# Selective-scan kernel: one three-set product on VectorE, a shared ring of three PSUM slots, five places for sets

## The chip, the cores and the metric

One core of a Trainium2 chip runs the whole program in one launch. The metric is device microseconds of that core; the time of a kernel is the median of its runs. A profile is one more execution of the same program, taken by the hardware profiler; its durations and waits belong to that execution and not to the median.

## What is computed

Two layers of a 2-D state-space block over 8 images of 64x64 positions and 96 channels. Each layer normalizes by groups of channels, projects 96 channels to 192 (and to 192 gates), convolves each channel 3x3, and then scans the 4096 positions in four directions (by rows, by columns, and both backward). Cut to what matters, layer 0's scan is, per direction, channel and one of 16 states:

```
delta = softplus(dt + bias)              # per position and channel
dA    = exp(delta * A)                   # the decay, one per state
h     = dA * h + delta * u * B[state]    # along the positions
y     = sum over states of h * C[state]
```

The four directions' y are added, normalized, gated and projected back. Layer 1 does the same with a form of the scan in which only the first 160 positions of a direction can matter for these inputs (its decays fall below any float after them); the kernel calls these *short* sets, and keeps a general second layer behind a test on the data that does not run here.

## The kernel before

**Tiling.** A *set* is 128 partitions by 1024 positions in float32: 32 channels times 4 of the 16 states. Four sets (`i` = 0 to 3) make a *group*: all 16 states of 32 channels. Three groups make a *job* (96 channels), two jobs a *unit* (192 channels, 1024 positions of one direction), and 16 units an image: 4 directions of 4 pieces. So an image has 96 groups and the program 768 groups of long sets, and 48 short sets (6 for each image).

**What one group costs each engine.** With lines as in the profile:

- ScalarE (ACT) writes each set's decay into a PSUM slot of 128x1024 (two banks): `fill`, L939. Once a group it copies delta\*u, which a DMA has spread over the partitions, into PSUM too: `drive`, L957. It also copies the finished sums out (`release`, L1074) and keeps the last state of each set (`keep_state`, L1003).
- VectorE (DVE) multiplies delta\*u by the tables of B, for sets 0 and 1 in one instruction of 128x2048 (L977) and for set 2 in one of 128x1024 (L979), and runs one scan instruction per set (L992), in place over the product.
- GpSimd (POOL) forms the product with B for set 3 (`early`, L965), and multiplies every scanned set by C into a tile `out` (`read_out`, L1008). Once a job it also forms delta\*u (`take_product`, L603).
- TensorE (PE) sums the four states in a partition group and the four sets into one PSUM bank (`collect`, L1035 and L1044), and in between does the projections, the softplus sums and the convolutions of other images (L573, L693, L727, L1111).
- SyncE (SP) issues the DMAs: `fetch` (L532) brings delta and delta\*u of each group, two groups ahead, 512 KB each; `replicate` (L543) brings the eight tables of B and C of a unit, 512 KB each.

**The products lie in a ring** of four places of one SBUF tile, `ring[:, i, :]`: set `i` of every group has place `i`. The tables lie in one SBUF tile, B's at 0 to 3 and C's at 4 to 7, and are overwritten in place at each new unit. `out` has 5 buffers.

**PSUM.** Eight banks: two decay slots (`pslot`, 2 buffers of two banks), one slot for delta\*u and for the short sets' gates (`pdrive`, two banks), one bank for the sums (`pacc`), one for everything else (`pmisc`).

**The order is written out by hand**: no scheduler moves an instruction, and each engine runs its instructions in the order in which the loop of `scan_rows` (L455) issues them. The loop steps over the sets; at the step of set n it issues

1. on SP, the fetch for the group that begins at set n+5;
2. on DVE, `advance_set` of set n: the products, if n is set 0 (L977) or set 2 (L979) of its group, and then the scan;
3. on ACT, `fill` of set n+1, then, if set n+2 begins a group, `drive` of that group; then `release` of the group that ended at set n-4, `keep_state` of set n-1, and `gate` of set n+1 if that is short;
4. on POOL, `read_out` of set n-1, and after it `early` of set n+2 if that is set 3 of its group;
5. on SP, the tables of the unit that begins at set n+4, n+3, ... n: B0 and B1 together four sets ahead, then C0 and B3, then C1 and B2, then C2, then C3, each after the last reader of the old table;
6. on PE, `collect` of set n-3, and a plan of stages of the next jobs, on all engines.

So on POOL a group's order is: read-out of set 0, product of set 3, read-outs of sets 1, 2 and 3; the job's `take_product` stands between the read-out of set 3 and the next group's read-out of set 0. The last scan of a group (set 3) needs POOL's product; each read-out needs its scan; a product on DVE needs the read-outs of what lay in its places; a fill needs the scan that last read its slot; a read-out needs the `collect` that last read its `out` buffer.

Of the kernel before, what the change touches and what calls it, by code (L numbers as in the profile page):

```python
# [9 lines left out]
F32 = mybir.dt.float32  # L10
AF = mybir.ActivationFunctionType
ALU = mybir.AluOpType
PSUM = bass.MemoryType.PSUM
# [8 lines left out]
T = 1024  # L22
# [3 lines left out]
P = 128  # L26
# [3 lines left out]
NG = C // GC  # L30
NS = N // GS
# [2 lines left out]
ROWS = R + 1 + 2 * N  # L34
PE_ROWS = 40
AHEAD = 5
SETS = 4
PER = NG * NS
HEAD = 160
HN = K * HEAD  # L40
# [5 lines left out]
HT = 2 * BLOCK  # L46
# [6 lines left out]
def two_ss2d_layers(ctx: ExitStack, tc: tile.TileContext, t: dict, out: bass.AP):  # L53
# [13 lines left out]
    nc = tc.nc  # L67
# [40 lines left out]
    for i in range(L // MM):  # L108
        at = slice(i * MM, (i + 1) * MM)
# [277 lines left out]
    def scan_parts(b):  # L387

        units, jobs, sets = [], [], []
        for k in range(K):
            order = range(NT) if k < 2 else range(NT - 1, -1, -1)
            for nth, i in enumerate(order):
                unit = dict(k=k, nth=nth, t0=i * T, column=k % 2 == 1, backward=k >= 2)
                unit.update(short=False, n=T)
                units.append(unit)
                for h in range(NH):  # L400
                    jobs.append(dict(unit=unit, h=h))
                    for g in range(NG):
                        group = dict(unit=unit, job=jobs[-1], h=h, g=g)
                        sets += [
                            dict(unit=unit, group=group, i=i, first=h == g == i == 0)
                            for i in range(NS)
                        ]
        if b >= 1:
            unit, more_jobs, more = short_parts(b - 1)
            units, jobs, sets = units + [unit], jobs + more_jobs, sets + more  # L410
        x_dbl = [dram.tile([2 * ROWS, L], F32, name=f"x_dbl{c}", bufs=2) for c in "rc"]
        return units, jobs, sets, x_dbl
# [12 lines left out]
    def scan_rows(xc, y, parts, plan, rows, beside):  # L425

        with (
            tc.tile_pool(name="loads", bufs=2, side="right") as loads,
            tc.tile_pool(name="piece", bufs=1) as piece,
            tc.tile_pool(name="work", bufs=2) as work,
            tc.tile_pool(name="pslot", bufs=2, space=PSUM) as pslot,  # L440
            tc.tile_pool(name="pdrive", bufs=1, space=PSUM) as pdrive,
            tc.tile_pool(name="pacc", bufs=1, space=PSUM) as pacc,
            tc.tile_pool(name="pmisc", bufs=1, space=PSUM) as pmisc,
        ):
            units, jobs, sets, x_dbl = parts
            total = len(sets)
            plan = plan(pmisc)
            with tc.manual_schedule():
                state = None
                arena = piece.tile([P, 4 * T], F32, name="arena")  # L450
                ring = work.tile([P, SETS, T], F32, name="set", bufs=1)
                tables = loads.tile([P, 2 * NS, T], F32, name="bc_rep", bufs=1)
                cums = cycle(tables[:, i, :] for i in (1, 3, 2, NS + 1))
                plan.setdefault(-1, []).insert(0, lambda: low_rows(x_dbl, units[1], rows))
                for n in range(-AHEAD, max(total + 4, max(plan, default=0) + 1)):  # L455
                    at = lambda i: sets[n + i] if 0 <= n + i < total else None
                    m, j = divmod(n + 1, PER)
# [12 lines left out]
                    fetch(at(AHEAD), False, loads, None)  # L470
                    fetch(at(2), True, loads, cums)
                    if at(0) and at(0)["unit"]["nth"] == 0 and at(0)["first"]:
                        state = piece.tile([P, D // GC * NS], F32, name="state0", bufs=2)
                    advance_set(at(0), state, ring, tables)
                    fill(at(1), pslot)
                    drive(at(2), pdrive)
                    release(at(-4), y, beside)
                    keep_state(at(-1))
                    gate(at(1), pdrive)
                    early(at(1), True, ring)  # L480
                    read_out(at(-1), work)
                    early(at(2), False, ring)
                    replicate(at(4), x_dbl, tables, ("b", 0), ("b", 1))
                    replicate(at(3), x_dbl, tables, ("c", 0), ("b", 3))
                    replicate(at(2), x_dbl, tables, ("c", 1), ("b", 2))
                    replicate(at(1), x_dbl, tables, ("c", 2))
                    replicate(at(0), x_dbl, tables, ("c", 3))
                    replicate_short(at(4), "b", tables[:, 0, :])
                    replicate_short(at(3), "c", tables[:, NS, :])
                    late = (n + 1) % NS == 0  # L490
                    if not late:
                        collect(at(-3), xc, y, pacc)
                    for stage in plan.pop(n, []):
# [444 lines left out]
        rate = w["a0"][:, rate : rate + 1]  # L938
        nc.scalar.activation(s["decay"], s["group"]["dt"], AF.Exp, scale=rate)  # L939

    def gate(s, pdrive):

        if s and s["unit"]["short"]:
            s["gate"] = pdrive.tile([P, T], F32, name="drive")[:, :HT]

            for i in range(NS):
                rate = w["a1_half"][:, column(s) + i :][:, :1]
                cum, out = blocks(s["group"]["cum"], i), blocks(s["gate"], i)  # L950
                nc.scalar.activation(out, cum, AF.Tanh, bias=half_log, scale=rate)  # L951

    def drive(s, pdrive):

        if s and s["i"] == 0 and not s["unit"]["short"]:
            s["group"]["drive"] = pdrive.tile([P, T], F32, name="drive")[:, : s["unit"]["n"]]
            nc.scalar.copy(s["group"]["drive"], s["group"]["dtu"])  # L957

    def early(s, short, ring):

        if s and by_gpsimd(s) and s["unit"]["short"] == short:
            nth = s["group"]["h"] * NG + s["group"]["g"] if short else s["i"]
            s["buf"] = ring[:, nth % SETS, : s["unit"]["n"]]
            b = s["unit"]["b", s["i"]]
            nc.gpsimd.tensor_tensor(s["buf"], s["group"]["dtu"], b, ALU.mult)  # L965

    def advance_set(s, state, ring, tables):
# [2 lines left out]
            return  # L970
        unit = s["unit"]
        if not by_gpsimd(s):
            i = s["i"]
            s["buf"] = ring[:, i, :]
            if i == 0:
                drive = s["group"]["drive"].unsqueeze(1).broadcast_to([P, 2, T])
                nc.vector.tensor_tensor(ring[:, :2, :], drive, tables[:, :2, :], ALU.mult)  # L977
            elif i > 1:
                nc.vector.tensor_tensor(s["buf"], s["group"]["drive"], unit["b", i], ALU.mult)  # L979
        if unit["short"]:  # L980
            buf = s["buf"]
            nc.vector.scalar_tensor_tensor(  # L982
# [21 lines left out]

    def read_out(s, work):
        if s:
            s["out"] = work.tile([P, T], F32, name="out", bufs=5)[:, : s["unit"]["n"]]
            nc.gpsimd.tensor_tensor(s["out"], s["buf"], s["unit"]["c", s["i"]], ALU.mult)  # L1008

    def collect(s, xc, y, pacc):  # L1010
# [239 lines left out]
    def scan_last(b, xc):  # L1250

        unit, jobs, sets = short_parts(b)
        with (
# [21 lines left out]
                            at, at, w["dsum1"][:, h : h + 1], None, ALU.mult  # L1275
                        )
            with (
                tc.tile_pool(name="pslot", bufs=2, space=PSUM) as pslot,
                tc.tile_pool(name="pdrive", bufs=1, space=PSUM) as pdrive,
                tc.tile_pool(name="pacc", bufs=2, space=PSUM) as pacc,  # L1280
                tc.manual_schedule(),
            ):
# [3 lines left out]
                for n in range(-4, len(sets) + 4):  # L1286
# [2 lines left out]
                    fetch(at(2), True, loads, cums)  # L1289
                    replicate_short(at(3), "c", tables[:, 1, :])  # L1290
                    advance_set(at(0), None, ring, tables)
                    fill(at(1), pslot)
                    gate(at(1), pdrive)
                    early(at(1), True, ring)
                    read_out(at(-1), work)
                    collect(at(-2), xc, xc, pacc)
# [760 lines left out]
```

## Time and profile before

| | |
|---|---|
| three runs | 11965.03, 11974.39, 11977.57 us; median 11974.39 us |
| the profiled execution | 11977.88 us, of which the span is 11976.1 us |
| granted TensorE clock, mean | 0.758 |
| first group of images 0 to 7 starts at | 138.0, 1506.9, 2984.7, 4455.5, 5919.7, 7391.5, 8855.7, 10320.8 us in the trace |
| image 2's scans, 2973.3 to 4231.0 us of the span: busy | DVE 1197.30, POOL 1181.86, ACT 980.63 of 1257.70 us |
| ACT fill (L939), mean of 3072 | 1114 ns |
| DVE scan with a carried state (L992), mean of 2304 | 2340 ns |
| DVE scan from zero (L992), mean of 768 | 2281 ns |
| POOL read-out (L1008), mean of 3072 | 2371 ns |
| POOL product for set 3 (L965), mean of 768 | 2419 ns |
| POOL delta\*u (L603), mean of 240 | 2644 ns |
| ACT drive (L957), mean of 768 | 1013 ns |

The page lists busy time by engine and the costliest groups of instructions, with the idle time of the engine ahead of them and what ended it. The view of waits totals, for each pair of lines, how long one waited for the other. The timeline lists instructions in order of time; equal neighbours are merged into one line with a count ("x2"), and a wait stands in brackets behind the instruction that it held up, with its releaser. A wait for several semaphores is put down to the one that came last.

### The profile page before, as it was taken

The page shows a single profiled execution, that of the slowest core. Times are in us where ns is not written, and L with a number is a line of the kernel's source. Part 1 is how long each engine was busy: PE and PEld are TensorE (multiplying, and loading weights), DVE is VectorE, ACT ScalarE, POOL GpSimd, SP SyncE. Part 2 cuts the span into 40 slices and gives each one's busy share as a digit, 9 for nine tenths or more (in the row PEclk, how much of TensorE's full clock was granted, in tenths as well). Part 3 has the DMA queues.
Part 4 walks back from the last instruction along what each step waited for, and adds up shares of the span by engine and source line. Part 5 has one row for each costly group of instructions (what it writes and reads, how often), then busy time and mean ns, then how long its engine had stood idle before and what let it go on. Part 6 is the DMA issues. An engine that isn't in the chain of part 4 may idle for free. (4 is left out here: it accounts for less than half of the span.)

```text
span 11976.1 us, 146959 instructions
## 1 busy us (share of the span) xinstructions
PE 8766.6 (73%) x50950; PEld 3994.0 (33%) x50950; DVE 10805.4 (90%) x6095; ACT 9033.1 (75%) x14768; POOL 10621.1 (89%) x4799
## 2 busy tenths in 40 slices
PE   6865577777877777877787777877677776886557
PEld 2332233332333323333233332333233332333322
DVE  8999899996999979999799987999879998899985
ACT  6777678776787767877778777787777877777775
POOL 6999799996999969999799987999879998799984
PEclk7776677777777777777777777777777877777667
DMA  4444444544445445444444445444544554444441
GB/s 132 154 167 156 130 160 165 166 161 146 159 160 167 161 146 170 165 159 156 150 165 165 167 145 162 164 156 167 166 144 166 167 166 160 143 155 164 157 147 62
DMA packets 670703, 1862.39 MB, mean 156 GB/s; under 512 B 186728, under 2 KB 201486, under 8 KB 669949
## 3 DMA queue, kind: packets, MB, share of 16 engines
q1 hardware_dynamic: 662781, 1840.30, 46.7%
q10 hardware_dynamic: 7168, 12.59, 0.3%
q8 instruction: 405, 6.64, 0.2%
q14 instruction: 349, 2.86, 0.1%
HBM read 1539.34 MB, written 313.28 MB: 155 GB/s over the span
## 5 line engine op out<-in xcount | busy, mean ns | idle before, releaser
L1008 POOL TENSOR_TENSOR out<-set,bc_rep 128x1024 f32<-128x1024 f32 x3120 | 7318.7, 2369 | 624.8 <-DVE set L992 531.0
L992 DVE TENSOR_TENSOR_SCAN set<-decay,state,set 128x1024 f32<-128x1024 f32 x2304 | 5322.6, 2340 | 314.5 <-ACT decay L939 172.3
L939 ACT ACTIVATE decay<-dt_rep,w_a 128x1024 f32<-128x1024 f32 x3072 | 3420.5, 1114 | 1277.0 <-DVE set L992 1272.3
L1044 PE MATMUL acc<-out,w_gather 128*32 128x256 f32 x24576 | 2405.7, 519 | 50.3 <-POOL out L1008 49.9
L1111 PE MATMUL ps_conv<-edged,taps 96*96 96x512 f32 (+1 forms) x4032 | 2222.8, 695 | 19.3 <-DVE arena L865 9.7
L965 POOL TENSOR_TENSOR set<-dtu_rep,bc_rep 128x1024 f32<-128x1024 f32 (+1 forms) x816 | 1966.4, 2410 | 70.8 <-DMA dtu_rep<-dtu_short 38.6
L992 DVE TENSOR_TENSOR_SCAN set<-decay,set 128x1024 f32<-128x1024 f32 x768 | 1731.4, 2281 | 122.6 <-ACT decay L939 60.6
L977 DVE TENSOR_TENSOR set<-drive,bc_rep 128x2048 f32<-128x2048 f32 x768 | 1743.4, 2270 | 35.7 <-DMA bc_rep<-x_dblr 24.1
L727 PE MATMUL ps_sp<-w_eye,arena 128*96 128x128 f32 x7680 | 1122.4, 309 | 584.2 <-ACT arena L739 489.3
L1035 PE MATMUL acc<-map,w_eye 96*32 96x256 f32 x4608 | 578.0, 585 | 1309.8 <-ACT map L1074 859.6
L1074 ACT COPY map<-acc 32x256 f32<-32x256 f32 x3072 | 1472.6, 479 | 68.7 <-PE acc L1044 27.9
L1044 PEld LDWEIGHTS acc<-out,w_gather 128*32 128x32 f32 x24576 | 880.5, 141 | 1435.3 <-issue 1043.0
L727 PEld LDWEIGHTS ps_sp<-w_eye,arena 128*96 128x96 f32 x7680 | 972.4, 144 | 893.1 <-ACT arena L739 607.7
L693 PE MATMUL ps_dt<-w_dtw,x_dbl 7*128 7x96 f32 x3840 | 832.8, 382 | 572.4 <-ACT arena L739 460.4
L1111 PEld LDWEIGHTS ps_conv<-edged,taps 96*96 96x96 f32 (+1 forms) x4032 | 708.3, 190 | 1305.9 <-issue 1249.8
L693 PEld LDWEIGHTS ps_dt<-w_dtw,x_dbl 7*128 7x128 f32 x3840 | 727.2, 279 | 821.1 <-ACT arena L739 530.0
L979 DVE TENSOR_TENSOR set<-drive,bc_rep 128x1024 f32<-128x1024 f32 x768 | 922.0, 1201 | 30.9 <-DMA bc_rep<-x_dblr 14.2
L957 ACT COPY drive<-dtu_rep 128x1024 f32<-128x1024 f32 x768 | 777.9, 1013 | 109.6 <-DMA dtu_rep<-dtu_far 85.0
L704 ACT ACTIVATE arena<-ps_dt 128x384 f32<-128x384 f32 x480 | 235.1, 490 | 580.2 <-PE ps_dt L693 552.3
L1035 PEld LDWEIGHTS acc<-map,w_eye 96*32 96x32 f32 x4608 | 104.3, 125 | 1631.2 <-ACT map L1074 1005.3
L603 POOL TENSOR_TENSOR arena<-arena,map 96x1024 f32<-96x1024 f32 x240 | 634.7, 2644 | 7.9 <-ACT arena L739 7.8
L1003 ACT COPY state<-set 128x1 f32<-128x1 f32 x2304 | 422.3, 183 | 6.8
(207 smaller groups left out, 7991.9 us busy)
## 6 DMA issues: line engine op xcount, KB each, us to landing
dt_rep<-dt_far SPq DMA_DIRECT2D x768, 512.0 KB
dtu_rep<-dtu_far SPq DMA_DIRECT2D x768, 512.0 KB
bc_rep<-x_dblr SPq DMA_DIRECT2D x512, 512.0 KB
bc_rep<-x_dblc SPq DMA_DIRECT2D x512, 512.0 KB
dt_far<-arena SPq DMA_DIRECT2D x240, 384.0 KB
dtu_far<-arena SPq DMA_DIRECT2D x240, 384.0 KB
xc_far<-conv_out SPq DMA_DIRECT2D x224, 192.0 KB
dt_rep<-dt_short SPq DMA_DIRECT2D x48, 480.0 KB
```

The lines of the kernel that those rows point to most:

```text
L693: nc.tensor.matmul(job["ps"][:, j, :], unit["x_dbl"][: R + 1, at : at + P], w["dtw0"][:, k, h * C : (h + 1) * C], start=True, stop=True,)
L727: nc.tensor.matmul(job["ps"][:C, j * P : (j + 1) * P], job[name][:, s * BLOCKS + j, :], w["whole_eye"], is_transpose=True, start=i == 0, s ...
L939: nc.scalar.activation(s["decay"], s["group"]["dt"], AF.Exp, scale=rate)
L957: nc.scalar.copy(s["group"]["drive"], s["group"]["dtu"])
L965: nc.gpsimd.tensor_tensor(s["buf"], s["group"]["dtu"], b, ALU.mult)
L977: nc.vector.tensor_tensor(ring[:, :2, :], drive, tables[:, :2, :], ALU.mult)
L979: nc.vector.tensor_tensor(s["buf"], s["group"]["drive"], unit["b", i], ALU.mult)
L992: nc.vector.tensor_tensor_scan(ordered(s["buf"], unit), ordered(s["decay"], unit), ordered(s["buf"], unit), 0.0 if unit["nth"] == 0 else s ...
L1008: nc.gpsimd.tensor_tensor(s["out"], s["buf"], s["unit"]["c", s["i"]], ALU.mult)
L1044: nc.tensor.matmul(acc, w["gather"], s["out"][:, at : at + n], start=False, stop=s["i"] == NS - 1, skip_group_check=True,)
L1074: nc.scalar.copy(yk, like(acc, unit["column"]))
L1111: nc.tensor.matmul(job["ps"][:C, :], taps[l][:k, h, tap, :], edged[:k, tap // 3 : tap // 3 + rows, tap % 3 : tap % 3 + WW], start=tap == 0 ...
```

## The change

- `pdrive` goes. `pslot` has three buffers of two banks, and decays, delta\*u (`drive`) and the short sets' gates all take their slots from it in turn. The order on ACT stays, except that for short sets `gate` is issued ahead of `fill`.
- DVE forms the products of sets 0, 1 and 2 in one instruction of 128x3072 at set 0. The instruction for set 2 alone (L979) goes: 768 instructions of 128x3072 stand where 768 of 128x2048 and 768 of 128x1024 stood.
- The ring has five places. POOL's product always uses place 4. DVE's three use places 1, 2, 3 in one group and 2, 1, 0 in the next, in turn, so that the product of a new group overwrites the places of sets 0 and 1 of the old group and a free place, and not the place of set 2.
- The table of B for set 2 is loaded four sets ahead of the unit, with those of sets 0 and 1, and no longer two sets ahead behind C1.
- `out` has 4 buffers in place of 5.
- The scan of the last image's short sets gets the same ring of slots and gate order.

```
-SETS = 4
+SETS = 5
+TRIPLE = (1, 2, 3), (2, 1, 0)
...
+                        group["odd"] = len(sets) // NS % 2
...
-            tc.tile_pool(name="pslot", bufs=2, space=PSUM) as pslot,
-            tc.tile_pool(name="pdrive", bufs=1, space=PSUM) as pdrive,
+            tc.tile_pool(name="pslot", bufs=3, space=PSUM) as pslot,
...
                     advance_set(at(0), state, ring, tables)
+                    gate(at(1), pslot)
                     fill(at(1), pslot)
-                    drive(at(2), pdrive)
+                    drive(at(2), pslot)
                     release(at(-4), y, beside)
                     keep_state(at(-1))
-                    gate(at(1), pdrive)
                     early(at(1), True, ring)
                     read_out(at(-1), work)
                     early(at(2), False, ring)
-                    replicate(at(4), x_dbl, tables, ("b", 0), ("b", 1))
+                    replicate(at(4), x_dbl, tables, ("b", 0), ("b", 1), ("b", 2))
                     replicate(at(3), x_dbl, tables, ("c", 0), ("b", 3))
-                    replicate(at(2), x_dbl, tables, ("c", 1), ("b", 2))
+                    replicate(at(2), x_dbl, tables, ("c", 1))
...
-            s["group"]["drive"] = pdrive.tile([P, T], F32, name="drive")[:, : s["unit"]["n"]]
+            s["group"]["drive"] = pslot.tile([P, T], F32, name="decay")
             nc.scalar.copy(s["group"]["drive"], s["group"]["dtu"])
...
-            nth = s["group"]["h"] * NG + s["group"]["g"] if short else s["i"]
-            s["buf"] = ring[:, nth % SETS, : s["unit"]["n"]]
+            nth = s["group"]["h"] * NG + s["group"]["g"]
+            place = (3, 2, 1, 0, 4)[nth % SETS] if short else SETS - 1
+            s["buf"] = ring[:, place, : s["unit"]["n"]]
...
         if not by_gpsimd(s):
-            i = s["i"]
-            s["buf"] = ring[:, i, :]
-            if i == 0:
-                drive = s["group"]["drive"].unsqueeze(1).broadcast_to([P, 2, T])
-                nc.vector.tensor_tensor(ring[:, :2, :], drive, tables[:, :2, :], ALU.mult)
-            elif i > 1:
-                nc.vector.tensor_tensor(s["buf"], s["group"]["drive"], unit["b", i], ALU.mult)
+            odd = s["group"]["odd"]
+            s["buf"] = ring[:, TRIPLE[odd][s["i"]], :]
+            if s["i"] == 0:
+                out = ring[:, 2::-1, :] if odd else ring[:, 1:4, :]
+                drive = s["group"]["drive"].unsqueeze(1).broadcast_to([P, NS - 1, T])
+                nc.vector.tensor_tensor(out, drive, tables[:, : NS - 1, :], ALU.mult)
...
-            s["out"] = work.tile([P, T], F32, name="out", bufs=5)[:, : s["unit"]["n"]]
+            s["out"] = work.tile([P, T], F32, name="out", bufs=4)[:, : s["unit"]["n"]]
```

More of the change, by code (lines that the diff above doesn't have):

```diff
@@ L939, in fill, with gate @@
         nc.scalar.activation(s["decay"], s["group"]["dt"], AF.Exp, scale=rate)
-    def gate(s, pdrive):
+    def gate(s, pslot):
         if s and s["unit"]["short"]:
-            s["gate"] = pdrive.tile([P, T], F32, name="drive")[:, :HT]
+            s["gate"] = pslot.tile([P, T], F32, name="decay")[:, :HT]
             for i in range(NS):
@@ L951, in gate, with drive @@
                 nc.scalar.activation(out, cum, AF.Tanh, bias=half_log, scale=rate)
-    def drive(s, pdrive):
+    def drive(s, pslot):
         if s and s["i"] == 0 and not s["unit"]["short"]:
-            s["group"]["drive"] = pdrive.tile([P, T], F32, name="drive")[:, : s["unit"]["n"]]
+            s["group"]["drive"] = pslot.tile([P, T], F32, name="decay")
             nc.scalar.copy(s["group"]["drive"], s["group"]["dtu"])
@@ L1277, in scan_last @@
             with (
-                tc.tile_pool(name="pslot", bufs=2, space=PSUM) as pslot,
-                tc.tile_pool(name="pdrive", bufs=1, space=PSUM) as pdrive,
+                tc.tile_pool(name="pslot", bufs=3, space=PSUM) as pslot,
                 tc.tile_pool(name="pacc", bufs=2, space=PSUM) as pacc,
@@ L1291, in scan_last @@
                     advance_set(at(0), None, ring, tables)
+                    gate(at(1), pslot)
                     fill(at(1), pslot)
-                    gate(at(1), pdrive)
                     early(at(1), True, ring)
```

## The prediction

> **What bounds the kernel now.** I read the page first, then the groups by shape, then the view of waits, then the timeline of DVE and of POOL over the same groups.
>
> ```profile
> PE 8766.6 (73%) x50950; PEld 3994.0 (33%) x50950; DVE 10805.4 (90%) x6095; ACT 9033.1 (75%) x14768; POOL 10621.1 (89%) x4799
> ...
> L977 DVE TENSOR_TENSOR set<-drive,bc_rep 128x2048 f32<-128x2048 f32 x768 | 1743.4, 2270 | 35.7 <-DMA bc_rep<-x_dblr 24.1
> ...
> L979 DVE TENSOR_TENSOR set<-drive,bc_rep 128x1024 f32<-128x1024 f32 x768 | 922.0, 1201 | 30.9 <-DMA bc_rep<-x_dblr 14.2
> ```
>
> DVE and POOL are equally full, so neither busy share says which of them sets the pace of a group. The two product rows give DVE's price: 1069 ns for each further 1024 columns, 1201 - 1069 = 132 ns for being an instruction of its own.
>
> ```profile
> DVE set L992 <- ACT decay L939: 232.9, 156, 8.5
> ```
>
> That is all DVE waits for decays in 3072 scans; on POOL's product the same scans wait 41.7 us (89 times). Now the order in time, DVE first, then POOL:
>
> ```profile
> 3304.80 2.29 DVE L977 TENSOR_TENSOR set<-drive,bc_rep 128x2048 f32<-128x2048 f32 x1
> 3307.20 4.47 DVE L992 TENSOR_TENSOR_SCAN set<-decay,set 128x1024 f32<-128x1024 f32 x2
> 3311.58 1.20 DVE L979 TENSOR_TENSOR set<-drive,bc_rep 128x1024 f32<-128x1024 f32 x1
> 3312.88 4.47 DVE L992 TENSOR_TENSOR_SCAN set<-decay,set 128x1024 f32<-128x1024 f32 x2
> ...
> 3330.31 2.27 DVE L977 TENSOR_TENSOR set<-drive,bc_rep 128x2048 f32<-128x2048 f32 x1
> 3332.68 4.47 DVE L992 TENSOR_TENSOR_SCAN set<-decay,set 128x1024 f32<-128x1024 f32 x2
> 3337.07 1.20 DVE L979 TENSOR_TENSOR set<-drive,bc_rep 128x1024 f32<-128x1024 f32 x1
> 3338.37 2.29 DVE L992 TENSOR_TENSOR_SCAN set<-decay,set 128x1024 f32<-128x1024 f32 x1
> 3341.35 2.29 DVE L992 TENSOR_TENSOR_SCAN set<-decay,set 128x1024 f32<-128x1024 f32 x1 [0.69 <-POOL set L965]
> ```
>
> ```profile
> 3309.63 2.36 POOL L1008 TENSOR_TENSOR out<-set,bc_rep 128x1024 f32<-128x1024 f32 x1 [0.17 <-DVE set L992]
> 3311.96 2.39 POOL L965 TENSOR_TENSOR set<-dtu_rep,bc_rep 128x1024 f32<-128x1024 f32 x1
> ...
> 3326.78 7.00 POOL L1008 TENSOR_TENSOR out<-set,bc_rep 128x1024 f32<-128x1024 f32 x3
> 3333.73 2.89 POOL L603 TENSOR_TENSOR arena<-arena,map 96x1024 f32<-96x1024 f32 x1
> 3336.57 2.36 POOL L1008 TENSOR_TENSOR out<-set,bc_rep 128x1024 f32<-128x1024 f32 x1
> 3338.89 2.43 POOL L965 TENSOR_TENSOR set<-dtu_rep,bc_rep 128x1024 f32<-128x1024 f32 x1
> ```
>
> In the first group POOL starts the read-out of set 0 as soon as scan 0 ends, then makes its product, done at 3314.35. DVE reaches scan 3 at about 3315.1: 0.7 us to spare. In the last group (the first of a job) the `take_product` has made POOL late, the product ends at 3341.32, and scan 3 waits for it. So a loop runs through both engines: scan 0, read-out 0, POOL's product, scan 3, next DVE product, scan 0. What keeps it off the path is the time DVE spends between scan 0 and scan 3: scan 1, **the single product**, scan 2.
>
> **The change part by part.**
>
> *The product.* By the rows DVE's instruction grows from 2270 to 2270 + 1069 = 3339 ns and 1201 ns go: 132 ns, and with the gaps around the single product (scan 1 to scan 2 is 3.54 us with it, 2.27 us without) 0.18 us a group, 138 us in all, if DVE set the pace. The Trainium skill says so: "Perfetto Trace Analysis", Identifying the Most-Contended Engine, has the engine with the highest occupancy optimized first, which here is DVE at 90%. By that rule the time would fall by those 138 us; the timeline above speaks against it. The skill's "Vector Engine (DVE) Microarchitecture Reference", Measured stream behaviour on trn2, gives about 75 ns per instruction; by it alone the saving would be an estimated 58 us.
>
> But 1.07 us of product moves from the slack side of the loop onto the loop. From the starts and ends of all 768 groups in the trace:
>
> - Scan 0's end to the end of POOL's product: 4.89 us where POOL isn't late (least 4.80). Handoff to scan 3: 0.03 us at the least.
> - Scan 3's start to the next scan 0's end: median 6.96 us, so 8.03 after the change.
> - DVE's own way from scan 0 to scan 3: 5.73 us now, 5.73 - 1.25 = 4.48 after. 4.48 < 4.89: scan 3 waits for POOL in every group without a conv product (L1124, 0.66 us, in the third group of most jobs) in between.
>
> So the loop takes 4.89 + 0.03 + 8.03 = 12.95 us (12.97 with its handoffs; 12.85 in the quarter of the groups whose scans start from zero), where DVE's undisturbed group now takes 12.69.
>
> I measure from end to end of POOL's product, because that is on the path in both kernels:
>
> - *First to second group of a job* (256 times): now mostly 12.0 us, as scan 3 follows at once. It must be 12.97: 216 of 256 lie below, by 180 us in sum.
> - *Second to third*: now mostly 12.69; 192 of 256 lie below, by 59 us in sum.
> - *Third to next first*: now 13.97 to 14.46, POOL back to back (three read-outs, `take_product`, read-out, product). Unchanged: what DVE gains there POOL doesn't pass on.
>
> 180 + 59 = **+239 us**. Against it: the 40 and 64 groups above the new length (by 73 and 137 us), where DVE waited for decays.
>
> *The ring of three.* By the order of allocations the fill of set 2 then waits for the DVE product and not for scan 0, the fill of set 3 for scan 0 and not for scan 1, the drive copy for scan 1 and not for the single product; those of sets 0 and 1 wait as before but have 1.07 us more. So a decay is due some 1.1 us later than it is ready now. If every wait above the new length shrinks by up to 1.2 us, the sum is +159; if DVE only saves its 0.18 there, +223; if in first groups ACT itself is the late one (it waits for PE's `ps_dt`, L704, 552 us in all, which no ring moves), +294. I take **+210**, nearest to the second.
>
> *B's table of set 2* comes two sets earlier, but the triple product needs all three at once. B1 has landed 4.5 us (median) before its reader; B2's landing is some 1.4 us later, as B1's is after B0's, and the reader comes 1.1 us earlier. 38 of 112 unit starts have under 2.5 us, short by 46 us in sum. The waits that the single product had for its table go (27.5 us), and 6 us are there already: **+12**, between -27 and +66. SP's queue loses one wait and gains none ahead of C0.
>
> *`out` with 4 buffers.* Read-out 0 would wait for PE's sum of the old group's set 0, which follows ACT's release. At today's times it is late in 227 of 768 groups, 199 us in sum, and POOL's product stands behind it. But that release follows scan 2 of the old group, and read-out 0 moves away from scan 2 by 1.07 us or more; by 0.5 us 106 us remain, by 1.5 us 12. I take **+10**, between 0 and 106.
>
> *Gates* in the shared ring: ACT is the bound there (fills 1.94 and gates 2.3 us a set, whichever first), 48 sets: 0, within 10 us either way. Product writes with a reversed order of places have no row; I price them as the forward ones, nearest by shape.
>
> Sum: +210 + 12 + 10 = +232 on the profiled execution's 11977.9 us, 12210; the median of the runs is 3.5 us lower: **12205 us**.
>
> **The rivals.**
>
> 1. *DVE sets the pace, and the ring frees ACT* (faster). Price: -138 us, and up to another 233 us of decay waits; 11974 - 138 = 11836. For it: 90% busy, 1272 us of ACT waiting for scans. It decides only if read-out 0 and POOL's product together take less than two scans (4.48 us); their rows say 2371 + 2419 ns and a handoff. Chance 0.07.
> 2. *Gain and loss cancel*: if the 73 + 137 us above the new length vanish wholly, 239 - 210 = +29 us are left, some 12000. For it: the fills do become earlier. Against: many of those waits are at the end of an image (5 to 7 us each), behind PE. 0.04.
> 3. *New waits on top*: ACT-bound first groups (+294), `out` (+106) and tables (+66) together: 11974 + 466 = 12440. For it: each alone was bounded so; against: the first delays POOL's readers and so relieves the second. 0.09.
> 4. That the change isn't what it says is excluded: the built program has 768 triple products, the order of the other instructions stands.
>
> **How the numbers follow.** The forecast has 0.80. Its own range is 12080 (159 - 27 - 10, less some 15 for rows) to 12380 (294 + 106, the ends that can meet); outside lie the rivals, 0.20. The measurement tells about 0.2% (24 us) from no change: faster 0.07, same 0.04, slower 0.80 + 0.09 = 0.89.
>
> **What would show it.** Scan rows' idle put on POOL's product (L965) should grow from 41.7 us to some 300, in most groups of a job's first two; triple products of 3.34 us x768; waits on decays fewer than 233 us; POOL's read-outs unchanged in length; groups of about 12.95 us in the middle of a job. It is wrong if POOL's product ends before DVE reaches scan 3, if a triple product is far from 3.34 us, or if POOL waits on PE for more than 100 us.

## The result and the profile after

The changed kernel takes **12289.85 us** (median of 4 runs, 12276.0 to 12304.38) against 11970.53 us (4 runs of the kernel before beside it): ratio 1.0268, 95% interval 1.0256 to 1.028. It is slower, by some 85 us more than forecast, and inside the range.

The profiled execution took 12288.49 us (span 12286.0 us, granted TensorE clock 0.756; before 0.758). All functions around the scan stand one or a few lines further down than before: the product is L980, the scan L993, POOL's product L967, the read-out L1009, the fill L940. Drive copies and gates now carry the name `decay` as well. First the page, busy times and then three groups with count, busy us, mean ns and the idle time ahead:

```profile
PE 8714.0 (71%) x50950; PEld 3940.2 (32%) x50950; DVE 10757.5 (88%) x5327; ACT 9046.4 (74%) x14768; POOL 10624.2 (86%) x4799
...
L1009 POOL TENSOR_TENSOR out<-set,bc_rep 128x1024 f32<-128x1024 f32 x3120 | 7330.7, 2375 | 881.9 <-DVE set L993 699.7
L993 DVE TENSOR_TENSOR_SCAN set<-decay,state,set 128x1024 f32<-128x1024 f32 x2304 | 5289.5, 2336 | 523.3 <-POOL set L967 367.2
...
L980 DVE TENSOR_TENSOR set<-decay,bc_rep 128x3072 f32<-128x3072 f32 x768 | 2577.6, 3356 | 60.3 <-DMA bc_rep<-x_dblr 35.2
```

DVE has 768 instructions and 48 us of busy time less, POOL has the same work as before (10621.1 us), and both are now idle longer. The view of waits (engine, tile and line, for what; us in total, times, longest us) says for whom:

```profile
DVE set L993 <- POOL set L967: 512.0, 509, 2.1
...
DVE set L993 <- ACT decay L940: 128.0, 40, 7.6
```

Scans waited 41.7 us for POOL's product before, and wait 512.0 us now, 509 times: about the first two groups of each of the 256 jobs. The waits for decays went down from 232.9 us. The timeline of DVE over one group in the middle of an image shows the loop closed:

```profile
2557.56 3.36 DVE L980 TENSOR_TENSOR set<-decay,bc_rep 128x3072 f32<-128x3072 f32 x1
2561.02 6.65 DVE L993 TENSOR_TENSOR_SCAN set<-decay,set 128x1024 f32<-128x1024 f32 x3
2568.23 2.29 DVE L993 TENSOR_TENSOR_SCAN set<-decay,set 128x1024 f32<-128x1024 f32 x1 [0.56 <-POOL set L967]
2570.54 3.36 DVE L980 TENSOR_TENSOR set<-decay,bc_rep 128x3072 f32<-128x3072 f32 x1
```

and POOL's beside it:

```profile
2563.46 2.37 POOL L1009 TENSOR_TENSOR out<-set,bc_rep 128x1024 f32<-128x1024 f32 x1 [1.24 <-DVE set L993]
2565.78 2.41 POOL L967 TENSOR_TENSOR set<-dtu_rep,bc_rep 128x1024 f32<-128x1024 f32 x1
```

Three scans follow each other behind the triple product. POOL has been idle for 1.24 us when it starts the read-out of set 0, right behind scan 0. It makes its product until 2568.19, and scan 3, which DVE could have begun 0.56 us earlier, starts at 2568.23. From product to product it is 12.98 us.

**Where the time went**, from the instruction times of the whole trace, between the ends of the last scans of successive groups (760 steps within images; 7 from one image to the next, where the short sets and the rest of the block lie; and the span's ends):

| us | within images | between images | rest of span | span |
|---|---|---|---|---|
| before | 10132.7 | 1304.1 | 539.3 | 11976.1 |
| after | 10370.1 | 1369.1 | 546.8 | 12286.0 |
| difference | +237.4 | +65.0 | +7.5 | +309.9 |

The first column is what the prediction summed up (+232 with its small terms). The other two, 72 us, it had at nothing. Of the seven steps between images the first has no short sets in it and takes 128.2 us against 127.7; the other six take 204.0 to 211.3 us against 194.6 to 197.3.

### The profile page after: what moved, and what is told of

It reads as the page before. It is cut to its first block, busy times and chain, and to the rows that moved or that the text cites. A ratio compares the mean times of both kernels' runs of the same rounds, so it can differ in the third digit from the quotient of the medians.

```text
span 12286.0 us, 145575 instructions
## 1 busy us (share of the span) xinstructions
PE 8714.0 (71%) x50950; PEld 3940.2 (32%) x50950; DVE 10757.5 (88%) x5327; ACT 9046.4 (74%) x14768; POOL 10624.2 (86%) x4799
## 5 line engine op out<-in xcount | busy, mean ns | idle before, releaser
L1009 POOL TENSOR_TENSOR out<-set,bc_rep 128x1024 f32<-128x1024 f32 x3120 | 7330.7, 2375 | 881.9 <-DVE set L993 699.7
L993 DVE TENSOR_TENSOR_SCAN set<-decay,state,set 128x1024 f32<-128x1024 f32 x2304 | 5289.5, 2336 | 523.3 <-POOL set L967 367.2
L940 ACT ACTIVATE decay<-dt_rep,w_a 128x1024 f32<-128x1024 f32 x3072 | 3417.0, 1113 | 644.3 <-DVE set L980 392.0
L980 DVE TENSOR_TENSOR set<-decay,bc_rep 128x3072 f32<-128x3072 f32 x768 | 2577.6, 3356 | 60.3 <-DMA bc_rep<-x_dblr 35.2
L1112 PE MATMUL ps_conv<-edged,taps 96*96 96x512 f32 (+1 forms) x4032 | 2198.2, 688 | 40.9 <-DVE arena L866 22.6
L967 POOL TENSOR_TENSOR set<-dtu_rep,bc_rep 128x1024 f32<-128x1024 f32 (+1 forms) x816 | 1961.7, 2404 | 110.3 <-DMA dtu_rep<-dtu_short 70.3
L993 DVE TENSOR_TENSOR_SCAN set<-decay,set 128x1024 f32<-128x1024 f32 x768 | 1722.4, 2278 | 202.1 <-POOL set L967 144.7
L728 PE MATMUL ps_sp<-w_eye,arena 128*96 128x128 f32 x7680 | 1175.9, 318 | 599.1 <-DVE conv_out L1125 312.3
L728 PEld LDWEIGHTS ps_sp<-w_eye,arena 128*96 128x96 f32 x7680 | 1014.9, 148 | 941.1 <-DVE conv_out L1125 471.9
L694 PE MATMUL ps_dt<-w_dtw,x_dbl 7*128 7x96 f32 x3840 | 760.8, 357 | 554.2 <-ACT arena L740 441.4
L958 ACT COPY decay<-dtu_rep 128x1024 f32<-128x1024 f32 x768 | 778.1, 1013 | 476.8 <-DVE set L993 355.6
L694 PEld LDWEIGHTS ps_dt<-w_dtw,x_dbl 7*128 7x128 f32 x3840 | 660.8, 255 | 783.3 <-ACT arena L740 504.5
L574 PE MATMUL ps_proj<-map,w_wx 96*78 96x512 f32 x512 | 409.5, 938 | 6.3 <-ACT x_dbl L585 2.8
## 6 DMA issues: line engine op xcount, KB each, us to landing
dt_rep<-dt_far SPq DMA_DIRECT2D x768, 512.0 KB
dtu_rep<-dtu_far SPq DMA_DIRECT2D x768, 512.0 KB
bc_rep<-x_dblr SPq DMA_DIRECT2D x512, 512.0 KB
bc_rep<-x_dblc SPq DMA_DIRECT2D x512, 512.0 KB
```

Source lines behind the costliest of these rows:

```text
L694: nc.tensor.matmul(job["ps"][:, j, :], unit["x_dbl"][: R + 1, at : at + P], w["dtw0"][:, k, h * C : (h + 1) * C], start=True, stop=True,)
L728: nc.tensor.matmul(job["ps"][:C, j * P : (j + 1) * P], job[name][:, s * BLOCKS + j, :], w["whole_eye"], is_transpose=True, start=i == 0, s ...
L980: nc.vector.tensor_tensor(out, drive, tables[:, : NS - 1, :], ALU.mult)
L993: nc.vector.tensor_tensor_scan(ordered(s["buf"], unit), ordered(s["decay"], unit), ordered(s["buf"], unit), 0.0 if unit["nth"] == 0 else s ...
L1112: nc.tensor.matmul(job["ps"][:C, :], taps[l][:k, h, tap, :], edged[:k, tap // 3 : tap // 3 + rows, tap % 3 : tap % 3 + WW], start=tap == 0 ...
```

## The experiments

The theory: within the images the loop of the prediction sets the pace, because the triple product stands between scan 3 and the next scan 0; between them the gate, issued ahead of the fill, delays the short sets. The rivals: the shared ring, the four buffers of `out`, or the tables that must come together. The table splits each profiled execution as above; medians are of 4 to 11 runs. One execution of a kernel differs from the next by up to 0.4% (49 us over 27 runs of the kernel before), and a split is that of one execution.

| kernel | median us | ratio to before [95%] | within | between |
|---|---|---|---|---|
| E1 cut 2+1 | 12626.4 | 1.0549 [1.0531, 1.0566] | 10713.4 | 1363.6 |
| E2 cut 1+2 | 12744.17 | 1.0648 [1.063, 1.0665] | 10840.1 | 1368.9 |
| E3 gate last | 12188.53 | 1.0193 [1.0176, 1.021] | 10338.4 | 1309.8 |
| E4 POOL's product earlier | 11922.84 | 0.9968 [0.9956, 0.9981] | 9979.9 | 1365.8 |
| E5 own banks | 12226.41 | 1.0222 [1.0205, 1.0239] | 10387.7 | 1326.7 |
| E6 own banks, cut 2+1 | 12705.15 | 1.0623 [1.0606, 1.0641] | 10841.2 | 1313.4 |
| E7 E3 and E4 together | 11843.89 | 0.991 [0.9894, 0.9927] | 9983.5 | 1305.8 |
| E8 before, POOL's product earlier | 11947.19 | 0.9991 [0.9981, 1.0] | 10114.0 | 1300.3 |
| E9 E6, table mended | 11993.98 | 1.0022 [1.0012, 1.0031] | 10137.1 | 1307.2 |
| E10 E1, table mended | 11981.74 | 1.0009 [0.9999, 1.0018] | 10057.8 | 1370.9 |
| E11 before, `out` 4 | 11995.88 | 1.0017 [1.0008, 1.0026] | 10146.9 | 1295.2 |
| E12 2+1, both ahead of scan 0 | 12223.03 | 1.0208 [1.0192, 1.0224] | 10303.6 | 1366.3 |

### E1, E2 and E6: the product cut, and a table fetched too early

E1 cuts the triple product of the changed kernel in two and moves one part behind scan 0; E2 cuts it the other way (set 0 at `i == 0`, sets 1 and 2 at `i == 1`):

```
             if s["i"] == 0:
-                out = ring[:, 2::-1, :] if odd else ring[:, 1:4, :]
-                drive = s["group"]["drive"].unsqueeze(1).broadcast_to([P, NS - 1, T])
-                nc.vector.tensor_tensor(out, drive, tables[:, : NS - 1, :], ALU.mult)
+                out = ring[:, 2:0:-1, :] if odd else ring[:, 1:3, :]
+                drive = s["group"]["drive"].unsqueeze(1).broadcast_to([P, 2, T])
+                nc.vector.tensor_tensor(out, drive, tables[:, :2, :], ALU.mult)
+            elif s["i"] == 1:
+                out = ring[:, TRIPLE[odd][2], :]
+                nc.vector.tensor_tensor(out, s["group"]["drive"], tables[:, 2, :], ALU.mult)
```

E6 is E1 on the kernel E5 (below), with a bank of its own for delta\*u.

> The changed kernel with its triple product cut in two: the products of sets 0 and 1 ahead of scan 0, that of set 2 alone between scan 0 and scan 1. Ring of three, four buffers of out, order of gates and tables stay. Theory (the loop): 1.07 us of product leaves the way from scan 3 to the next scan 0 and gives DVE back its way of 5.7 us from scan 0 to scan 3, longer than POOL's 4.9; scans' idle on POOL's product falls from 512 us to under 120, groups within the images get some 240 us shorter in sum, the 60 us between the images stay: 12050 us (12000 to 12110). Rival (the shared ring, the four buffers or the tables that come together make the loss): nothing of theirs is undone, the time stays within 30 us of 12290, or rises by 0.13 to 0.18 us a group, 100 to 138 us, as there is one instruction more.

> The changed kernel with its triple product cut the other way: the product of set 0 ahead of scan 0, those of sets 1 and 2 in one instruction between scan 0 and scan 1. Theory (the loop): the way from scan 3 to the next scan 0 shrinks by 2.1 us against the triple product instead of 1.07, but already with 1.07 the loop was off the path, and DVE's own 12.7 us a group or POOL's work set the end: within 40 us of the other cut, some 12050 us (12000 to 12110). Rival (what the product costs is proportional to where it stands, without a threshold): another 240 us less, some 11800. Rival (ring, buffers, tables): within 30 us of 12290, or 100 to 138 us above.

> As the kernel with banks of their own, and the triple product cut: sets 0 and 1 ahead of scan 0, set 2 alone between scan 0 and scan 1. The cut was slower in the shared ring (12626 us), where the fill of set 2 takes the bank that the single product still reads. Theory (the loop, and in the shared ring that new wait): with a bank of its own for delta*u the wait is gone, the way from scan 3 to the next scan 0 is 6.96 us again, and groups within the images take what they took before the change, within 40 us; with four buffers of out and the tables 0 to 30 us more than before: 11980 us (11930 to 12030). Rival (the cut itself costs, whatever the banks): above 12400. Rival (out and tables make the loss): 12150 to 12250.

All three got slower, by 336, 454 and 479 us against their uncut partners, far above what the theory expected. E1 and E2 lie outside the numbers of their rivals too; E6 fits the number of its rival that the cut itself costs (above 12400). E6's profile has the reason; its view of waits, DVE's rows:

```profile
DVE set L984 <- DMA bc_rep<-x_dblc: 375.1, 64, 10.6
DVE set L984 <- DMA bc_rep<-x_dblr: 333.6, 56, 10.4
```

The cut product (L984 there) waits 120 times, 708.7 us in sum, for a table of B, and all of E6's loss lies from the second to the third group of a job (697 us more than E5 there, and less than E5 in the other two steps). In the changed order the tables of sets 0, 1 and 2 of the next unit are fetched at the step of set 0 of a unit's last group, behind the triple product that read them. A product of set 2 one step later comes after that fetch: it waits for the transfer and, in these three kernels, uses the next unit's table in the last group of a unit. So the runs say nothing of the loop. They do show what the change's fetch order rests on: the table of set 2 can be fetched that early only because no product of set 2 follows the triple. E2 was not run again; whether a further 1.07 us off the loop is worth anything was not tried.

### E9 and E10: the cut product with its table behind the last reader

```
-                    replicate(at(4), x_dbl, tables, ("b", 0), ("b", 1), ("b", 2))
-                    replicate(at(3), x_dbl, tables, ("c", 0), ("b", 3))
+                    replicate(at(4), x_dbl, tables, ("b", 0), ("b", 1))
+                    replicate(at(3), x_dbl, tables, ("c", 0), ("b", 3), ("b", 2))
```

E9 is E6 with this edit, E10 is E1 with it.

> The kernel with banks of its own and the cut product once more, with one thing mended: in the three cut kernels so far the table of B for set 2 was fetched for the next unit ahead of the cut product of the unit's third group, which so waited some 700 us in sum for that transfer and read the next unit's table. Here that table is fetched one set later, behind its last reader. Theory (the loop): 10841 us less those 709 us of waits leaves 10132 us within the images, what the kernel before takes; with 1313 between them and 560 around them 12005 us (11950 to 12040), some 220 under the same kernel with the triple product. Rival (the cut itself costs): above 12200.

> The changed kernel, shared ring and gates as changed, with the product cut and the table of set 2 fetched behind its last reader. Theory (the loop): the triple product alone makes the loss within the images, so most of 240 us goes, and the 65 us between the images stay: 11990 us (11900 to 12070). Rival (the shared ring makes the loss, or opens one as the fill of set 2 now waits for the single product behind scan 0): 12200 or more.

11994 us and 11982 us, both within 12 us of the theory's number. Within the images E9 takes 10137 us where E5, the same kernel with the triple product, takes 10388, and E10 takes 10058 where the changed kernel takes 10370. So **moving 1.07 us of the product from ahead of scan 0 to behind it is worth 251 and 312 us**, without and with the shared ring (232 and 308 us by the medians). Both kernels have the four buffers of `out`, and E10 has the shared ring. Both also fetch the table of set 2 a step later, but DVE's idle time ahead of its products, 60.3 us in the changed kernel, is still 36.0 + 4.7 us in E10, so the tables can account for some 20 us at most. The place of the triple product makes the loss within the images, and the rivals there fall. DVE's and POOL's rows in E9's view of waits are worth a look:

```profile
DVE set L997 <- POOL set L968: 290.6, 264, 2.6
...
POOL out L1013 <- PE acc L1049: 345.6, 258, 3.9
```

E9 waits longer for POOL's product than the kernel before (41.7 us) and POOL waits much longer for PE (40.0 us before), and yet its time within the images is within 5 us of before's. Long totals of waits are no price by themselves.

The ring shows its own worth here: E10 is 79 us shorter within the images than E9. The 64 us by which it is longer between them go with the order of the gates, which is the changed one in E10 and the old one in E9 (E3, below).

### E4 and E8: POOL's product a step earlier

One edit, in the changed kernel (E4) and in the one before (E8), so that POOL's order in a group is product, read-outs 0, 1, 2, 3:

```
-                    early(at(2), False, ring)
+                    early(at(3), False, ring)
```

> The changed kernel with one edit: POOL issues its product for set 3 one step earlier, behind read-out 3 of the group before and ahead of read-out 0. Theory (the loop): read-out 0 is no longer between scan 0 and scan 3, so the loop is gone; scans' idle on POOL's product falls from 512 us to under 60. What is left is POOL's own work, per job 12 read-outs of 2.37, 3 products of 2.42 and the map's 2.89, 38.6 us, against some 41.0 now, and DVE's, 3 x 12.5 us: up to 2 us a job less in 256 jobs: 11800 us (11750 to 11950), below the kernel before. Rival (ring, buffers or tables): the order on POOL does not matter to them, within 50 us of 12290. Rival (the product takes the read-out's place: a later read-out 0 makes PE, the release and the next groups' banks late): 12100 to 12250.

> The kernel before the change with one edit: POOL's product for set 3 a step earlier, ahead of read-out 0. Theory (the loop): it binds before the change only in the groups where POOL is late, so little is to be had, DVE then sets 12.7 us a group, and waits for decays stay: 11900 us (11850 to 11960). The changed kernel with POOL's product earlier and the gate last should stand below it, by up to the 138 us that the triple product saves on DVE. Rival (POOL's earlier product is worth the same some 370 us in both kernels, and the triple product has nothing to do with it): 11600.

E4: 11923 us, 390 us less within the images than the changed kernel, and 0.3% faster than the kernel before. E8: 11947 us, 19 us less within the images than the kernel before. The same edit is worth twenty times more with the triple product. Read-out 0 is no longer ahead of POOL's product, and in E4's view of waits the row of scans on POOL's product is gone; among the long sets' rows these lead instead:

```profile
DVE set L993 <- ACT decay L940: 166.8, 106, 8.1
...
DVE set L980 <- POOL out L1009: 115.7, 150, 3.9
```

The second is a new wait that the edit opens: read-outs end later, and a triple product waits for a place. It comes, as one of the rivals has it, from a later read-out 0, and is far smaller than what went.

### E3 and E5: gates and banks

E3 puts the gate of the changed kernel back behind the release; all slots stay shared:

```
-                    gate(at(1), pslot)
                     fill(at(1), pslot)
                     drive(at(2), pslot)
                     release(at(-4), y, beside)
                     keep_state(at(-1))
+                    gate(at(1), pslot)
```

E5 has E3's order, and two buffers of `pslot` with a `pdrive` for drive and gates as before:

```
-            tc.tile_pool(name="pslot", bufs=3, space=PSUM) as pslot,
+            tc.tile_pool(name="pslot", bufs=2, space=PSUM) as pslot,
+            tc.tile_pool(name="pdrive", bufs=1, space=PSUM) as pdrive,
```

> The changed kernel with the gate of a short set put back behind the fill, the drive copy and the release; all three still take their banks from the shared ring. Theory (between the images the gate ahead of the fill holds the slot of dt_rep, and so SP's queue and the next loads): of the some 60 us that the 7 boundaries got longer, 40 to 60 go, groups within the images stay within 10 us: 12235 us (12215 to 12260). Rival (four buffers of out make the loss between the images: read-outs wait there for PE): the order of the gates is worth nothing, 12290 within 15 us.

> The changed kernel with the banks as before: two for decays, one of its own for delta*u and gates, the gate behind the fill while scans run. The triple product, five places, four buffers of out and the tables stay. Theory (the loop): the triple product still stands between scan 3 and the next scan 0, so the 240 us within the images stay, up to 60 more as the decays of sets 2 and 3 again wait for scans 0 and 1; the 60 us between the images go: 12215 us (12180 to 12300). Rival (the shared ring makes the loss): some 11975 within 30 us.

E3 gains 101 us by the medians, where the theory expected 30 to 75. Of the 99.5 us between the two profiled executions' spans, 59 are between the images and 8 in the rest of the span. The other 32 are spread over the images. POOL's instructions sum to 30 us less in that execution (its product takes 2384 ns in place of 2414), for which I have no cause; the same edit between E4 and E7 moves the time within the images by 4 us, so I do not count the 32 as an effect of the gates. The loss between the images is thus the order of the gates: four buffers of `out` stay in E3, and 1309.8 us there is close to before's 1304.1. In the table, the kernels with the gate first (E1, E2, E4, E10, E12) have 1363.6 to 1370.9 us between the images, and those with the gate last (E3, E5, E6, E7, E9) 1305.8 to 1326.7. What the gates did is in the view of waits, for before, after and E3: ACT's fill of a short set (`decay`, L935 before, L936 after) waiting for the transfer of delta, and its instruction for the gate (L951 before, L952 after; its tile is named `drive` before) waiting for that of the cumulated delta, `cum`:

```profile
ACT decay L935 <- DMA dt_rep<-dt_short: 41.5, 13, 5.7
...
ACT drive L951 <- DMA bc_rep<-cum_short: 4.8, 8, 1.4
```

```profile
ACT decay L952 <- DMA bc_rep<-cum_short: 92.1, 31, 10.4
```

```profile
ACT decay L936 <- DMA dt_rep<-dt_short: 33.4, 12, 5.6
...
ACT decay L952 <- DMA bc_rep<-cum_short: 12.4, 12, 2.5
```

With the gate first, ACT stands before a transfer that hasn't landed, and the fill behind it waits too; it has no wait for its own data left in that profile. The two rows sum to 46.3 us before, 45.8 in E3 and 92.1 in the changed kernel, so they hold some 46 of the 72 us. The likely reason that the transfer is late as well: the fill is the last reader of a delta buffer, and SP fetches in order, so a late fill holds back the next loads, `cum` among them. That second half is argued from the order in the code, not tested by itself.

E5, 12226 us, is in line with the loop: within the images it loses 255 us against before, though the PSUM slots and the order of the gates are as they were there. Of 22.6 us between its images I have no account; 9.4 of them lie in one step, and E6 and E9, with the same slots and gates, have 1313.4 and 1307.2 us there.

### E7: both gains together

> The changed kernel with both edits that gained: POOL's product a step earlier and the gate back behind the fill. Theory (two causes in two places, the loop within the images and the gates between them): the gains add, groups within the images as with POOL's product earlier alone (9980 us in sum), the stretches between and behind the images as with the gate last alone (1310 and 391): 11840 us (11810 to 11880). Rival (the gates only move a wait that the earlier product opens again): 11900 or more.

11844 us against the 11840 expected: the gains add, as they lie in different stretches. **E7 is faster than both kernels**; it takes 0.9% less than the one before (0.991 [0.9894, 0.9927]). Against E8, the old products with the same order on POOL, it is 103 us faster by the medians and 130 us within the images. So the triple product and the ring do save what DVE's rows promise, some 0.17 us a group, once the loop is off the path.

### E11: four buffers of `out` in the kernel before

```
-            s["out"] = work.tile([P, T], F32, name="out", bufs=5)[:, : s["unit"]["n"]]
+            s["out"] = work.tile([P, T], F32, name="out", bufs=4)[:, : s["unit"]["n"]]
```

> The kernel before the change with one edit: four buffers of out in place of five. Forecast of this term: +10 us, between 0 and 106. Theory (the loop, with the loss between the images from the gates): POOL's read-outs wait some more for PE, most of it where POOL has 0.8 us to spare: 0 to 30 us above the kernel before in the same call. Rival (four buffers make the changed kernel's loss): 100 us or more above it.

Ratio 1.0017 [1.0008, 1.0026], 25 us by the medians. The two profiled executions differ by 1.8 us in all, 14 more within the images and 12 less outside them. The rival falls. Two rows of its view of waits, DVE's and POOL's:

```profile
DVE set L992 <- POOL set L965: 113.7, 168, 1.9
...
POOL out L1008 <- PE acc L1044: 251.9, 195, 4.8
```

POOL waits 212 us longer for PE than before and passes on 72 us to the scans. Within the changed kernel the term was not taken out by itself; E9 and E10 have four buffers too, and within the images they take 4 us more and 75 us less than the kernel before.

### E12: two instructions where the triple stands

```
                 drive = s["group"]["drive"].unsqueeze(1).broadcast_to([P, 2, T])
                 nc.vector.tensor_tensor(out, drive, tables[:, :2, :], ALU.mult)
-            elif s["i"] == 1:
                 out = ring[:, TRIPLE[odd][2], :]
```

That is E1's cut, with both parts ahead of scan 0 (so no product follows the fetch of a table).

> The changed kernel with the triple product written as two instructions, both ahead of scan 0: the same work in the same place, with one instruction more per group. It gives the price of an instruction of its own there, by the rows 132 ns. Theory (the loop runs through DVE's product): 0.13 us in the two thirds of the groups in which the loop binds, 68 us, up to 0.18 us in all of them, 138 us: 12380 us (12345 to 12430). Rival (POOL's own work sets the pace, DVE only waits for it): 12290 within 20 us.

Both were wrong: 12223 us, **67 us less** than with one instruction. The timeline of DVE in E12, once around:

```profile
2582.42 2.29 DVE L980 TENSOR_TENSOR set<-decay,bc_rep 128x2048 f32<-128x2048 f32 x1
2584.63 1.21 DVE L982 TENSOR_TENSOR set<-decay,bc_rep 128x1024 f32<-128x1024 f32 x1
2585.76 6.83 DVE L995 TENSOR_TENSOR_SCAN set<-decay,state,set 128x1024 f32<-128x1024 f32 x3
```

From the start of the products to scan 0 it is 3.34 us, against 3.46 with the triple in the timeline further up (2557.56 to 2561.02). The single product starts before the double's recorded end (2584.71), and scan 0 before the single's (2585.84). Over all 768 groups the median start of scan 0 is 84 ns ahead of the end of the single product, which it does not read; behind the triple it is 104 ns after the end (103 to 105 ns in 695 of 768 groups). Whoever reads what the instruction directly ahead has written comes 188 ns later, and that is more than an instruction of its own costs. 0.123 us in the 512 groups in which the loop binds make 63 us. So the pace does follow what stands between scan 3 and scan 0, as the theory had it, but the price I had for an instruction was the wrong one.

## Why the prediction was right, and where it was off

- **The loop: right.** Scans wait for POOL's product in two of three groups, and undoing the triple (E9, E10) or taking the read-out out of the loop (E4) gives the time back. The sign was sized too low: the scans' idle on POOL's product was put at some 300 us and came to 512. From end to end of POOL's product, first to second group, 13.04 us is the median where 12.97 was forecast: the triple takes 3356 ns and not 3339, and it follows scan 3 by 43 ns more than products followed scans before (at the median 40 ns ahead of its recorded end, not 83). The third group's step to the next first is unchanged, 14.32 us (even groups) and 14.37 us (odd) on average against 14.29 and 14.32, as forecast.
- **Its net price: near.** +237 us within the images stand against +232. By pairs of groups it came out as +206 (first to second, forecast 180 ahead of relief), +26 (second to third, 59) and +10 (third to first, 0), measured at POOL's product, +242 in all. That the sum came so near is partly luck, as the first pair lies above its forecast and the second below. The ring's relief is not what made the second pair smaller: E5, without the shared ring, has +211, +27 and +19. Between E10 and E9 the ring's relief is 79 us; with the triple product in place (after against E5) it is 18, less than two executions differ by.
- **B's table: small.** +12 was taken, from -27 to +66; the idle time ahead of DVE's products went from 35.7 + 30.9 to 60.3 us, 6 us less. What it is worth in the kernel's time was not tried by itself.
- **`out` with four buffers: the right order of size.** +10 forecast; in the kernel before, E11, it is +25 by the medians and +14 within the images. The sign I named for being wrong, over 100 us of POOL waiting on PE, did occur (126.7 us) and meant little: E9 has 345.6 us of it at no cost in the images. It was badly chosen.
- **The gates: the step that failed.** "ACT is the bound there ..., whichever first, 48 sets: 0, within 10 us either way". ACT's two times do add up in either order; what I left out is that the two instructions wait for different transfers, and that the one put first was not ready. 65.0 + 7.5 us followed, 1.5 us a set, and E3 brings 68 of them back. They are most of the 85 us by which the forecast fell short; the remainder is smaller than what two executions differ by.
- **Reversed places cost nothing**: the triple takes 3356.9 ns in even and 3355.7 ns in odd groups.
- **The rule that spoke against it.** By the Trainium skill, "Perfetto Trace Analysis", Identifying the Most-Contended Engine, the engine with the highest occupancy comes first. With DVE relieved, the groups within the images took 237 us more, 2.0% of the span, as DVE shared a loop with an engine that was as full; with the loop opened on POOL's side the same relief is worth 103 us (E8 to E7).

## What to carry to other kernels

Where two engines are equally full, follow the handoffs in a circle and ask on which side of them a moved instruction lands; busy time saved on one engine counts only off that circle, and a reordering on the other engine may be what lets it count. Ahead of an instruction moved to the front of an in-order queue, look at what it waits for and not only at how long it runs. And before two loads are put together, the last reader of each buffer has to stand ahead of both.

## What the runs showed of the hardware

- On DVE an instruction that reads what the one directly ahead of it wrote starts 104 ns after that one's recorded end; one that does not, and waits for nothing else, starts 78 to 84 ns before it (medians). The same pair of instructions shows both: the single product and the scan behind it stand 104 ns apart in the kernel before, where it is the scan of that product, and overlap by 83 ns in E10, where it is the scan of another set (medians of 768). Putting another product in between took the 188 ns away, and two instructions were faster than one by 0.12 us.
- The Trainium skill, "VectorE: DVE Perf Modes", The DRAIN you can't avoid, has eight copies take the same time with a semaphore after each and with one at the end only. It does not say whether one copy reads what another wrote. In these traces consecutive instructions are not alike in this: the dependent ones stand further apart, by the 188 ns above.
- A triple product of 3072 columns reading PSUM and SBUF took 3356 ns, 1071 ns for each 1024 columns beyond the 1214 ns of a single one in E12.
